# Convolution results of later chunks kept in DRAM, adapter weights brought on chip before the adapters

## The chip, the core and the metric

The kernel runs on one core of one Trainium2 chip. The core has a matrix engine (PE; PEld is its weight load), a vector engine (DVE), an activation engine (ACT), a general engine (POOL) and SP, which here only issues DMAs. DMAs are issued on the queues of SP, ACT and POOL, each of which takes its instructions in order, and all of them run on the same 16 DMA engines. The metric is the device time of one execution in microseconds (us).

## The reference

Four residual layers are applied one after the other to x of shape (32, 64, 1024), in float32. Cut to what matters:

```python
x = x + L0(x)   # per channel h: causal convolution with K_h of 1024 taps, plus D_h * x; masked by length
x = x + einsum('bsi,boi->bso', x, W1[id1])   # one 1024 x 1024 adapter out of 16 for each batch
x = x + einsum('bij,bkj->bik', x, W2[id2])   # and a second one
x = x + L3(x)   # gated FFN, 1024 -> 2752 -> 1024, each product with a rank-16 addition by id3
...
K = 2.0 * einsum('hn,hnl->hl', Ct, exp(dtA[:, :, None] * arange(length))).real
...
gate = lora_add(einsum('bnh,fh->bnf', x, W_gate), x, A_gate, B_gate)
up = lora_add(einsum('bnh,fh->bnf', x, W_up), x, A_up, B_up)
act = silu(gate) * up
down = lora_add(einsum('bnf,hf->bnh', act, W_down), act, A_down, B_down)
```

The batch is 32 rows b with 64 tokens (h in the first layer) of 1024 values. The first layer convolves along the 1024 values, for each h with a kernel of its own, for all 32 rows at once; the later layers multiply along them.

## The kernel before

**Tiling.** x is held transposed, with 128 of the 1024 values on the partitions: a tile `[128, 8, 512]` holds one chunk of 8 batch rows (2 MB), and there are four chunks c = 0 to 3. The convolution works on all chunks at once, four channels (`ha`) at a time; everything after it goes chunk by chunk.

**Convolution** (`convolution`). `kernels(g)` computes the taps of eight channels on DVE, ACT and POOL, PE multiplies them together (`pk`), POOL adds D in the `ks` row (L754) and ACT writes them to DRAM (`kp`). `convolve` loads `uf` (the reversed x of four channels, 512 KB) and twice `hk` (overlapping rows of the taps of two channels, 1 MB, three buffers) on SP, PE makes 64 matmul instructions of them (L782, `pc`), DVE masks the result into `tmp`, and POOL adds `tmp` into the four chunks of x with four instructions (L798). All four chunks are therefore loaded at the start (L581) and lie on chip through the convolution; the last two lie in `x2pool`.

**Adapters** (`adapter`, `adapters`). A piece is one layer of one batch row: eight weight tiles of 512 KB (`early` or `wa`, kt = 0 to 7) are loaded on SP, PE makes 16 matmul instructions with each (L176, `pa`), DVE transposes the sum and adds it to x (L187, L189). A chunk has 16 pieces. Layer 1 of row b stands in front of layer 2 of row b - 1. The row's weight index is read by SP into a register; the read for a piece is held behind the loads of four pieces before. The tiles of chunk 0 first take `early` (nine tiles of their own) and then `wpool`, a pool of nine slots that the weights of the FFN share. `issue_after(blocks[5])` holds the first three pieces' loads behind the sixth `hk` load; after that the scheduler places them among the `hk` loads by its own estimate.

**FFN** (`ffn`, `gated`). For each chunk, hidden columns are worked off in blocks of six and five tiles m. A tile m has two halves g (gate and up, weights `wg` and `wu`), each of seven products on PE (L367, `pf`), with a low-rank addition (`pe`, L309) from rows gathered by POOL (`bgu`, L214). After each half, `between(i)` with i = 2m + g is called; it calls `other`, which gives out the 16 adapter pieces of the next chunk in even shares between the FFN's products, so that their weight loads run beside FFN work. After each block come the products of the down projection (L507, `po`), with weights `wd`. The order on PE is the program's; the scheduler places the instructions of the other engines.

**Chunks.** `xpool` has two x tiles. In the first `between` of chunk 0 POOL writes chunks 2 and 3 to DRAM (`park`, L124), and `x2pool` is given to `apool`, the FFN's activations. In the first `between` of chunk 1 (and 2) SP loads chunk 2 (and 3) back (L454, `x<-xd`) into the tile of chunk 0 (and 1); it waits there until ACT's `out_y` writes of the old chunk have read it.

## Time and profile before

| What | us |
|---|---|
| median of the 3 runs (2449.39 to 2451.61) | 2451.41 |
| the profiled execution's own time | 2448.96 |
| its span | 2447.3 |
| first to last convolution matmul (L782) | 41.5 to 206.4 |
| first to last adapter matmul of chunk 0 (L176) | 206.4 to 371.8 |
| first FFN matmul of chunks 0, 1, 2, 3 | 380.4, 926.5, 1471.5, 2020.1 |

The profile records one execution. Its page gives the busy time of each engine, the busy tenths of the span in 40 slices, the DMA queues with packets, bytes and the share of 16 engines that their packets took, the chain of waits that ended last, and the costliest groups of instructions with the idle time before them and what ended it. Queries of the trace give the same for a window, a tile or a source line; a timeline merges runs of like instructions: start, length, engine, line, operation, count, and in brackets the engine's idle time before and what ended it. `SPq` and `POOLq` are queues, where the time is that of issuing. A granted clock of 1.00 is the full clock of PE.

### The profile page before, as it was taken

Reading aid. Unit: us, or ns where it says so; the run is one execution under the profiler, and the core shown is the slowest. Engines: PE = TensorE matmul, PEld = TensorE weight load, DVE = VectorE, ACT = ScalarE, POOL = GpSimd, SP = SyncE. Lnnn points to the kernel's source line nnn. Section 1 sums busy time; section 2 is a strip of 40 time slices with the busy share of each in tenths; the row PEclk is TensorE's granted clock in tenths of the full one; section 3 lists DMA queues with packets and bytes.
Section 4 is the critical chain, followed back from the end, with each engine's and each line's share of the span. In section 5 each row is a group of like instructions: output and inputs, shape, how many; then the busy total and the mean of one; then the engine's idle time right before and its main releaser. Section 6 shows DMA issues by size and latency. Waiting matters only on the chain.

```text
span 2447.3 us, 47048 instructions
## 1 busy us (share of the span) xinstructions
PE 2353.5 (96%) x19488; PEld 1877.8 (77%) x19488; DVE 1166.1 (48%) x2264; ACT 313.2 (13%) x613; POOL 204.0 (8%) x286
## 2 busy tenths in 40 slices
PE   3898888999999999999999999999999999999999
PEld 3896336888877787877877787878877788888887
DVE  8811114544345544544344544544354545654554
ACT  3200002111011101110011101110011102110110
POOL 3533001000000020000000020000000020000000
PEclk9999999999999999999999999999999999999999
DMA  6789998565567547565566547565566543323221
GB/s 238 253 292 366 408 408 336 190 236 168 190 224 254 181 146 266 209 217 182 175 244 231 179 152 258 207 216 190 177 244 218 184 149 113 89 76 111 87 65 61
DMA packets 162967, 501.24 MB, mean 205 GB/s; under 512 B 19842, under 2 KB 53954, under 8 KB 161730
## 3 DMA queue, kind: packets, MB, share of 16 engines
q1 hardware_dynamic: 146338, 461.76, 54.2%
q0 software_dynamic: 9504, 27.80, 3.4%
q10 hardware_dynamic: 6912, 8.69, 1.0%
q8 instruction: 153, 2.51, 0.4%
q14 instruction: 60, 0.49, 0.1%
HBM read 485.29 MB, written 12.88 MB: 204 GB/s over the span
## 4 chain that ended last, share of the span: by engine, by line
PE 87%; issue 6%; DMA 3%; DVE 2%; POOL 0%; POOLq 0%; SPq 0%; ACT 0%; DVEq 0%; ACTq 0%
PE pf L367 43%; PE po L507 22%; PE pa L176 14%; PE pc L782 5%; PE pe L309 2%; PE pl_d L266 1%; PE po L292 1%; DMA x<-xd 1%; DMA early<-in_w 0%; DMA wf<-in_wu 0%; POOL x L798 0%; DMA out_y<-x 0%; DMA hk<-kp 0%; DMA raw_g<-in_ag 0%; DMA ln<-in_lens 0%
## 5 line engine op out<-in xcount | busy, mean ns | idle before, releaser
L367 PE MATMUL pf<-xd,wf 128*128 128x256 f32 (+1 forms) x2816 | 667.3, 381 | 0.0
L367 PEld LDWEIGHTS pf<-xd,wf 128*128 128x128 f32 (+1 forms) x2816 | 523.0, 187 | 89.1 <-issue 7.5
L176 PE MATMUL pa<-wa,x 128*32 128x256 f32 x8048 | 472.5, 384 | 33.9 <-DMA wa<-in_w 26.7
L367 PE MATMUL pf<-xd,s 128*128 128x256 f32 (+1 forms) x2112 | 499.2, 379 | 2.9 <-ACT c L383 1.7
L367 PEld LDWEIGHTS pf<-xd,s 128*128 128x128 f32 (+1 forms) x2112 | 395.8, 188 | 63.6 <-ACT c L383 2.1
L176 PEld LDWEIGHTS pa<-wa,x 128*32 128x32 f32 x8048 | 249.5, 111 | 249.8 <-DMA wa<-in_w 67.4
L507 PE MATMUL po<-act,wd 128*128 128x256 f32 x704 | 177.0, 385 | 0.0
L507 PE MATMUL po<-actd,s 128*128 128x256 f32 x704 | 172.9, 379 | 0.0
L507 PE MATMUL po<-actd,wd 128*128 128x256 f32 x704 | 172.9, 379 | 0.0
L782 PE MATMUL pc<-uf,hk 128*128 128x256 f32 (+7 forms) x1024 | 153.4, 313 | 17.0 <-DMA hk<-kp 16.7
L214 POOL DMA_INDIRECT bgu<-in_bgu,rows x44 | 45.9, 1044 | 1431.7 <-PE pe L309 1428.2
L782 PEld LDWEIGHTS pc<-uf,hk 128*128 128x128 f32 x1024 | 148.8, 196 | 21.3 <-DMA hk<-kp 9.6
L392 DVE TENSOR_TENSOR c<-pf,u 128x256 f32<-128x256 f32 (+1 forms) x88 | 37.4, 425 | 266.3 <-PE pf L367 266.3
L507 PEld LDWEIGHTS po<-act,wd 128*128 128x128 f32 x704 | 130.6, 190 | 28.0 <-issue 10.2
L507 PEld LDWEIGHTS po<-actd,s 128*128 128x128 f32 x704 | 133.6, 190 | 18.4
L507 PEld LDWEIGHTS po<-actd,wd 128*128 128x128 f32 x704 | 133.6, 190 | 18.4
L319 ACT COPY lt<-pe 128x512 f32<-128x512 f32 (+1 forms) x176 | 90.3, 598 | 372.8 <-PE pe L309 268.9
L337 DVE TENSOR_TENSOR s<-wf 128x512 f32<-128x512 f32 x88 | 59.9, 681 | 119.7 <-DMA wf<-in_wu 44.9
L396 DVE TENSOR_TENSOR c<-c,lt 128x1024 f32<-128x1024 f32 (+1 forms) x88 | 107.7, 1224 | 6.7
L187 DVE STREAM_TRANSPOSE y<-pa 128x512 f32<-128x512 f32 x64 | 45.5, 711 | 137.1 <-PE pa L176 137.1
L337 DVE TENSOR_TENSOR s<-wd 128x384 f32<-128x384 f32 x64 | 33.4, 521 | 137.5 <-PE po L507 97.4
L388 DVE TENSOR_TENSOR c<-pf,c 128x256 f32<-128x256 f32 (+1 forms) x88 | 37.3, 424 | 105.4 <-PE pf L367 105.2
(150 smaller groups left out, 1713.6 us busy)
## 6 DMA issues: line engine op xcount, KB each, us to landing
wa<-in_w SPq DMA_DIRECT2D x503, 512.0 KB, 7.6
wf<-in_wg SPq DMA_DIRECT2D x88, 512.0 KB, 4.4
wf<-in_wu SPq DMA_DIRECT2D x88, 512.0 KB, 5.2
wd<-in_wd SPq DMA_DIRECT2D x96, 384.0 KB, 4.5
hk<-kp SPq DMA_DIRECT2D x32, 1024.0 KB, 7.9
x<-in_xt SPq DMA_DIRECT2D x4, 2048.0 KB, 10.6
uf<-in_xf SPq DMA_DIRECT2D x16, 512.0 KB, 6.1
wd<-in_wd SPq DMA_DIRECT2D x32, 256.0 KB, 3.4
```

The lines of the kernel that those rows point to most:

```text
L176: nc.tensor.matmul(acc[i * S : (i + 1) * S, s * 256 : (s + 1) * 256], xs[c][:, kt, lo + s * S : lo + (s + 1) * S], wt[:, i * 256 : (i + 1) ...
L187: nc.vector.transpose(y, acc)
L214: nc.gpsimd.indirect_dma_start(out=t, out_offset=None, in_=table, in_offset=bass.IndirectOffsetOnAxis(ap=rows[:, c, piece : piece + 1], axis=0
L309: nc.tensor.matmul(ps[:n, at_ : at_ + 2 * H], bt[pair(j), g, i, :n], tms["gu"[g]][pair(j)], start=(g + i == 0), stop=True, skip_group_chec ...
L319: nc.scalar.copy(lt[:n, :, 2 * H * j : 2 * H * (j + 1)], ps[:n].rearrange("p (i t) -> p i t", i=4),)
L337: nc.vector.tensor_add(s1, a21, a22)
L367: nc.tensor.matmul(ps, ws[j][:, kt, :n], xb[j][:, kt, :], start=start and kt == 0, stop=kt == KH - 1, skip_group_check=True,)
L388: nc.vector.tensor_add(cq[:n, 3], pb, cq[:n, 3])
L392: nc.vector.tensor_add(cq[:n, 1], pb, u[:n])
L396: nc.vector.tensor_add(cf, cf, lt[:n, g].rearrange("p i t -> p (i t)"))
L507: nc.tensor.matmul(pss[j], ws[j][:k, i, :], ab[m - m0][j], start=(m == m0 and home[j] % 2 == 0), stop=(m == m1 - 1), skip_group_check=True,)
L782: nc.tensor.matmul(ps[:, j, d * B :], hk[:, j, d * P : (d + 1) * P], uf[:, i + j, : KT - d, :].rearrange("p k b -> p (k b)"), start=(d == ...
```

## The change

Chunks 1 to 3 are no longer loaded at the start. For each four channels POOL adds the convolution's result into chunk 0 only; the results of the other three chunks are copied by POOL into `co` (768 values per partition) and written by POOL's queue to `cd` in DRAM, in rows of 256 values. When a chunk's turn comes, `bring` loads its x from the input (2 MB, SP) and its results in four tiles `cv` of 512 KB that take slots of `wpool`; POOL adds them to x in 16 instructions. `bring` is called in two parts, in `between(0)` and `between(1)` of the chunk before, and `other` gives out the 16 pieces from `between(2)` on. `park` and the reload are gone.

The adapter loads become one stream (`weights`) in the order of the pieces. `fetch` draws from it: at `ha` = 0 the 20 tiles that have places of their own (16 in `early`, four in the x tile that chunk 1 takes later), and from `ha` = 12 on one more for each four channels, until nine more stand in `wpool`: 29 in all. The ids are loaded first on SP. `apool` is opened before the FFN.

In the built program SP's order at the start is: ids, `par`, `cst`, `ln`, x of chunk 0, the first `uf`, 20 weight tiles, and then the first `hk`. Of the nine later tiles three stand around the `hk` loads of `ha` = 4, and one each near those of `ha` = 24, 28, 32, 36, 40 and 44. At the start of chunks 1 and 2, SP issues two `wg`, two `cv`, two `wu`, two `cv`, one `wg`, x, one `wg`, and then the first eight `wa`, of which the first four wait for POOL. POOL has the gather of the second `bgu` ahead of the 16 adds there; for chunk 1 (in the FFN of chunk 0) it stands behind the first four adds, and four of the eight `raw_d` loads of the second block stand behind the first eight.

```diff
-EARLY = 9
+EARLY = 16
+HA = 4
...
-    def x_tile(pool, c, tag):
-        return pool.tile([P, KT, TC], F32, tag=tag, name=f"x{c}")
+    def x_tile(c):
+        return xpool.tile([P, KT, TC], F32, tag="x", name=f"x{c}")
     ctx.enter_context(tc.manual_schedule(engines={PE}))
-    xs = [x_tile(xpool, c, "x") for c in range(2)]
-    right = ExitStack()
-    x2pool = right.enter_context(tc.tile_pool(name="x2pool", bufs=1, side="right"))
-    first = right.enter_context(ExitStack())
+    place = x_tile("_early")
+    xs = [x_tile(0)]
+    first = ExitStack()
     epool = first.enter_context(tc.tile_pool(name="epool", bufs=1, side="right"))
-    late = [x_tile(x2pool, c, f"x{c}") for c in range(2, NCK)]
     early = [epool.tile([P, L], F32, tag=f"e{i}", name=f"early{i}") for i in range(EARLY)]
-    blocks = convolution(tc, cst, consts, xt, xf, ssm, lens, xs + late, ps_tile)
-    parked = []
-    def park():
-        for c, x_c in enumerate(late, 2):
-            d = dpool.tile([P, KT, TC], F32, tag=f"xd{c}", name=f"xd{c}")
-            nc.gpsimd.dma_start(d, x_c)
-            parked.append(d)
+    early += [
+        place[:, i : i + L // TC].rearrange("p k t -> p (k t)")
+        for i in range(0, KT, L // TC)
+    ]
+    cd = dpool.tile([NCK - 1, P, H // HA, HA * KT * BC], F32, tag="cd", name="cd")
     ids_sb = cpool.tile([1, 3 * B], I32, tag="ids", name="ids_sb")
     nc.sync.dma_start(ids_sb, ids)
+    loads = []
+    def layers(c):
+        for b in range(c * BC, (c + 1) * BC + 1):
+            if b < (c + 1) * BC:
+                yield 0, b
+            if b > c * BC:
+                yield 1, b - 1
+    def weights():
+        for layer, b in (at_ for c in range(NCK) for at_ in layers(c)):
+            with ExitStack() as after:
+                if len(loads) > 3:
+                    after.enter_context(tc.issue_after(loads[-4]))
+                e = nc.values_load(
+                    ids_sb[0:1, layer * B + b : layer * B + b + 1],
+                    engines=[SP],
+                    min_val=0,
+                    max_val=NE - 1,
+                )
+            for kt in range(KT):
+                name = f"wa{layer}_{b}_{kt}"
+                wt = early.pop(0) if early else wpool.tile([P, L], F32, tag="w", name=name)
+                w = (w1, w2)[layer]
+                load = nc.sync.dma_start(
+                    wt, w[bass.ds(e, 1), kt].rearrange("e p f -> p (e f)")
+                )
+                if kt == KT - 1:
+                    loads.append(load.ins)
+                yield wt
+    stream = weights()
+    ahead = []
+    def fetch(ha):
+        if ha == 0:
+            ahead.extend(next(stream) for _ in range(len(early)))
+        elif ha > HG and len(ahead) < EARLY + 4 + 9:
+            ahead.append(next(stream))
+    convolution(tc, cst, consts, xt, xf, ssm, lens, xs[0], cd, ps_tile, fetch)
+    def bring(c, part):
+        if part == 0:
+            xs.append(x_tile(c))
+            with tc.issue_after(loads[2 * BC - 1]):
+                nc.sync.dma_start(xs[c], xt[:, c])
+        n = H // HA // 4
+        for q in (2 * part, 2 * part + 1):
+            t = wpool.tile([P, n, HA * KT * BC], F32, tag="w", name=f"cv{c}_{q}")
+            nc.sync.dma_start(t, cd[c - 1][:, q * n : (q + 1) * n])
+            for g in range(n):
+                h = (q * n + g) * HA
+                xv = xs[c].rearrange("p k (b h) -> p k b h", h=H)[:, :, :, h : h + HA]
+                tv = t[:, g].rearrange("p (i k b) -> p k b i", k=KT, b=BC)
+                nc.gpsimd.tensor_tensor(xv, xv, tv, ALU.add)
...
-    def adapter(w, layer, b):
+    def adapter(layer, b):
         c, lo = b // BC, (b % BC) * H
-        with ExitStack() as after:
-            if len(loads) > 3:
-                after.enter_context(tc.issue_after(loads[-4]))
-            e = nc.values_load(
-                ids_sb[0:1, layer * B + b : layer * B + b + 1],
-                engines=[SP],
-                min_val=0,
-                max_val=NE - 1,
-            )
         acc = ps_tile(f"pa{layer}_{b}")
         for kt in range(KT):
-            name = f"wa{layer}_{b}_{kt}"
-            wt = early.pop(0) if early else wpool.tile([P, L], F32, tag="w", name=name)
-            load = nc.sync.dma_start(
-                wt, w[bass.ds(e, 1), kt].rearrange("e p f -> p (e f)")
-            )
+            wt = ahead.pop(0) if ahead else next(stream)
...
     def adapters(c):
-        for b in range(c * BC, (c + 1) * BC + 1):
-            if b < (c + 1) * BC:
-                yield adapter(w1, 0, b)
-            if b > c * BC:
-                yield adapter(w2, 1, b - 1)
-    with tc.issue_after(blocks[5]):
-        pieces = adapters(0)
-        for _ in range(3):
-            next(pieces)
-    for _ in pieces:
+        for layer, b in layers(c):
+            yield adapter(layer, b)
+    for _ in adapters(0):
         pass
     first.close()
...
-        def other(share, of=2 * FM * AT_GATED + (2 * KH - 3) * AT_DOWN):
+        def other(share, of=2 * (FM - 1) * AT_GATED + (2 * KH - 3) * AT_DOWN):
             due[0] += share * NPIECE
             while due[1] * of < due[0]:
                 next(others, None)
                 due[1] += 1
         def between(i):
-            if i == 0 and c == 0:
-                with tc.issue_after(cols[-1]):
-                    park()
-                right.close()
-                apools.append(
-                    ctx.enter_context(
-                        tc.tile_pool(
-                            name="apool", bufs=MB, side="right", reuse_waits="tile"
-                        )
-                    )
-                )
-            if i == 0 and c and c + 1 < NCK:
-                x_n = x_tile(xpool, c + 1, "x")
-                nc.sync.dma_start(x_n, parked[c - 1])
-                xs.append(x_n)
-            other(AT_GATED)
+            if i < 2:
+                if c + 1 < NCK:
+                    bring(c + 1, i)
+            else:
+                other(AT_GATED)
...
-def convolution(tc, cst, consts, xt, xf, ssm, lens, xs, ps_tile):
+def convolution(tc, cst, consts, xt, xf, ssm, lens, x0, cd, ps_tile, fetch):
...
-        for c in range(NCK):
-            nc.sync.dma_start(xs[c], xt[:, c])
+        nc.sync.dma_start(x0, xt[:, 0])
...
         def convolve(kp, row, ha):
-            uf = s3.tile([P, 4, KT, B], F32, tag="uf", name=f"uf{ha}", bufs=2)
-            nc.sync.dma_start(uf, xf[:, ha : ha + 4])
-            tmp = s2.tile([P, 4, KT * B], F32, tag="tmp", name=f"tmp{ha}")
-            for i in range(0, 4, 2):
+            uf = s3.tile([P, HA, KT, B], F32, tag="uf", name=f"uf{ha}", bufs=2)
+            nc.sync.dma_start(uf, xf[:, ha : ha + HA])
+            fetch(ha)
+            tmp = s2.tile([P, HA, KT * B], F32, tag="tmp", name=f"tmp{ha}")
+            for i in range(0, HA, 2):
...
-            tv = tmp.rearrange("p i (k b) -> p k b i", b=B)
-            for c in range(NCK):
-                xv = xs[c].rearrange("p k (b h) -> p k b h", h=H)[:, :, :, ha : ha + 4]
-                nc.gpsimd.tensor_tensor(xv, xv, tv[:, :, c * BC : (c + 1) * BC, :], ALU.add)
+            xv = x0.rearrange("p k (b h) -> p k b h", h=H)[:, :, :, ha : ha + HA]
+            tv = tmp.rearrange("p i (k b) -> p k b i", b=B)[:, :, :BC, :]
+            nc.gpsimd.tensor_tensor(xv, xv, tv, ALU.add)
+            co = s2.tile([P, NCK - 1, HA * KT, BC], F32, tag="co", name=f"co{ha}")
+            tv = tmp.rearrange("p i (k c b) -> p c (i k) b", k=KT, b=BC)[:, 1:]
+            nc.gpsimd.tensor_copy(co, tv)
+            nc.gpsimd.dma_start(
+                cd.rearrange("c p g e -> p c g e")[:, :, ha // HA],
+                co.rearrange("p c i b -> p c (i b)"),
+            )
```

## The prediction

> **What bounds the kernel now.** I read the busy shares first, then the windows by stage, then the timelines of the SP queue and of PE around the places that the diff touches.
>
> ```profile
> PE 2353.5 (96%) x19488; PEld 1877.8 (77%) x19488; DVE 1166.1 (48%) x2264; ACT 313.2 (13%) x613; POOL 204.0 (8%) x286
> DMA  6789998565567547565566547565566543323221
> ```
>
> 96% is an average over unlike stages. The windows below (columns: window, length, busy time of PE, PEld, DVE, ACT, POOL, then granted clock, DMA share, GB/s) separate them.
>
> ```profile
> 150.00:190.00 40.00, 39.97 (x298) 38.93 (x295) 6.00 (x9) 0.72 (x2) 14.44 (x20) 1.00 0.86 287
> 240.00:280.00 40.00, 33.42 (x502) 13.41 (x504) 5.63 (x8) 0.00 (x0) 0.00 (x0) 1.00 1.03 408
> ```
>
> The convolution (150 to 190 us) is bound by PE, with the DMA engines at 0.86. The first adapters (206 to 371 us) are bound by transfers: 408 GB/s at a DMA share of 1.03, and that is the ceiling I use. The FFN stages afterwards are PE again. The weight stream of the first adapters, and its last tile:
>
> ```profile
> 193.27 5.51 SPq L171 DMA_DIRECT2D early<-in_w  x7
> 201.53 159.38 SPq L171 DMA_DIRECT2D wa<-in_w  x119
> 370.72 1.07 PE L176 MATMUL pa<-wa,x 128*32 128x256 f32 x16 [0.21 <-DMA wa<-in_w]
> ```
>
> Only 2 of the 9 `early` tiles are issued before 193 us (117.7 and 155.7 in the SP timeline); 126 of the 128 tiles of 512 KB cross in this one stage. Two further holes in PE are the reloads of chunks 2 and 3:
>
> ```profile
> 941.42 7.11 PE L176 MATMUL pa<-wa,x 128*32 128x256 f32 x128 [2.59 <-DMA x<-xd]
> 1487.16 9.94 PE L176 MATMUL pa<-wa,x 128*32 128x256 f32 x128 [3.31 <-DMA x<-xd]
> ```
>
> The second piece also takes 9.94 instead of 7.11 us: the window 1470 to 1500 has a granted clock of 0.89, so the wait cost 3.3 us and another 2.9.
>
> **The change, part by part**, against the profiled execution's own 2448.96 us (span 2447.3, 1.7 around it).
>
> *A, 29 tiles ahead.* A tile takes 524,288 B / 408 GB/s = 1.285 us of DMA; a piece of 128 matmuls is 7.04 us in the chain of waits, so PE eats a tile in 0.88 us. In the new order of SP, 20 loads stand before the first `hk`, 9 more between the `hk` of ha = 4 and ha = 44. PE begins the adapters at 208.2 us as now (it waits there for the last add to chunk 0). The other 99 tiles need `wpool`'s 9 slots, which hold tiles 20 to 28; the first slot comes free when PE has passed tile 20, at 208.2 + 21 x 0.88 = 226.7. So the stream restarts at 226.7 instead of running on from 193.3: 126 tiles become 99 (27 x 1.285 = 34.7 saved), 33.4 us of early start are given up, and the gathers and low-rank loads that share the stream now (24% of it from 215 to 232 us), the last `hk` and ring slots not yet free lose their price, because they fall before the restart. Counted directly: first tile landed about 3.3 us after 226.7, then 98 x 1.285, gives 356; now 370.7. **-14** (bounds -11, if 3 us of today's disorder return, and -16).
>
> *B, chunk 1's first two pieces moved behind the first hidden tile.* Now chunk 0's first `m` runs from 380.44 to 422.62: 42.2 us, of which 24.4 + 2 x 7.04 = 38.5 is work; the weights `wu` are issued at 394.8, behind 8 `wa`. In the new order they follow 2 `wg`, `x1` and 2 `cv`: 10 units of 512 KB, some 13 us after the last adapter tile, and PE asks for them some 22 us after it. **-3** (0 to -3.7).
>
> *C, x brought in two parts, adapters one `m` later.* The x load still waits for the `out_y` writes (issue at 933.51 now, landing 7.8 us later). The first piece of the next chunk now runs 12.3 + 12.3 + 1.1 + 12.3 = 38 us after the chunk's start at 926.5, at 964.2. Before it, POOL must make 16 adds, rows of
>
> ```profile
> L798 POOL TENSOR_TENSOR x<-x,tmp x64: 828/858/1631, 58.0 to 209.7; 128x256 f32<-128x256 f32 x64
> ```
>
> from 941.3: 16 x 0.858 = 13.7, ready at 955; at the mean of that group (0.924) 956. 8 us to spare, so both waits go: 2.6 + 3.3 + 2.9 = **-8.8**. Queued behind: on POOL the gather of the next `bgu`, which stands ahead of the adds for chunks 2 and 3, and after four of them for chunk 1 (wanted by PE 20 us later); on SP the first four `wa`, which wait for POOL to release the `cv` slots, and behind them `wu` of m = 1 (needed at 971). Four of nine slots are held until 955, so I put +1 for small waits (0 to +7). The 12 `cv` and 3 x loads (12 MB) replace 4 MB of reload and 6 MB at the start, and the 4 MB parked from POOL's queue: these stages run at DMA shares of 0.5 to 0.7, so the cover is PE; without it the 24 units of 512 KB, against 8 of the reload, would cost 16 x 1.285 / 3 = 6.9 us a chunk. If x is late again, the first piece of the chunk is what waits.
>
> *D, POOL in the convolution.* Four adds become one add, one copy of 768 elements and a DMA issue. This POOL work is on the path once, where PE idles for the second kernel (7.2 us):
>
> ```profile
> 58.00 4.58 POOL x L798 x4
> 62.58 0.23 POOL ks L754
> 62.83 1.53 DMA kp<-ks
> 64.38 6.16 DMA hk<-kp
> ```
>
> No row shows a POOL copy. Between one 256-element operation with contention (1.15) and three of them uncontended (2.57) or contended (3.45): I take 2.5, as 768 elements are three of these rows. 1.15 + 2.5 = 3.65 for 4.58: **-0.9** (-2.3 to 0). The DMA issue stands behind the `ks` add.
>
> *E, the convolution's transfers.* Per four channels (9.25 us of PE) `hk` and `uf` take 0.855 x 9.25 = 7.9 us of DMA less the share of other queues, some 7.7. Six of the periods get a tile (+1.29), all get a 393 KB store in 384 rows of 1 KB. Its price is not in the trace; the rows around it are the queues of ACT's `out_y` (872 to 890 us) and of POOL's small loads (215 to 232 us); the columns are packets, MB, share:
>
> ```profile
> q10 hardware_dynamic: 288, 0.52, 7.6%
> ```
>
> ```profile
> q0 software_dynamic: 602, 1.55, 24.2%
> ```
>
> 7.6% of 18 us x 16 engines / 288 is 76 ns for 1.8 KB, the other 109 ns for 2.6 KB; by bytes alone 1 KB is 0.96 us a store, at 109 ns it is 2.6. Stores in 2 KB rows are nearest: scaled by size, some 46 ns, 1.1 us. 7.7 + 1.29 + 1.1 = 10.1 against a ceiling of 1.026 x 9.25 = 9.5: 0.6 x 6 = 3.6, less the 1.3 us by which an `hk` (lands in 7.9) is ahead of its use (two halves, 9.2): **+2.3** (0 to +19). The 20 loads, 10.5 MB from some 9 us on at 408 GB/s, end near 36 us, about when the first `hk` is issued (35.34): **+0.5** (0 to +8, at the 238 GB/s of the first slice).
>
> [...]
>
> [...]
>
> **Sum:** -14 - 3 - 8.8 + 1 - 0.9 + 2.3 + 0.5 = -22.9: 2426.1 us. The profiled execution is 2.45 below the median of the runs shown (2451.41) and 0.4 below the lowest (2449.39); I add 1 and say **2427**.
>
> **Rivals.**
> 1. *The convolution becomes bound by transfers.* A store costs 109 ns a row, 2.6 us: the six periods with a tile take 11.6 instead of 9.5 (+12.6), the other nine 10.3 (+7), less 1.3: +18 in place of +2.3, **2443**. For it: the share is 0.86 already. Against: 109 ns is of rows twice as long or more.
> 2. *The 20 loads hold up the first `hk`* (the slice's 238 GB/s): +8 instead of +0.5, **2435**. For it: nothing else can shift 41.5 us. Against: that slice was not saturated (share 0.6).
> 3. *The slower one: POOL's adds gate the chunk.* They are now between x's landing and the first piece, and hold four of nine weight slots, with SP waiting behind them. At t us an add they end at 941.3 + 16t, and `wu` lands some 10 us later (7 tiles); PE wants it at 971.3, so there is slack up to t = 1.25. At the row's maximum (1.63) each of two chunks loses 6 us and 2.9 of clock: 18 in all, still a little faster. From t = 1.8 the loss passes 22.9 and the change is slower; at t = 2.3 each loses 17 + 2.9: **2466**. For it: the same adds rose to 1.63 beside a busy DVE. Against: DVE was 97% busy there and is 48% here, and from 100 us on they average 0.885.
> 4. *The change doesn't do what it says*: the 9 later tiles get no slot before the adapters. 9 x 1.285 less the earlier restart: within 5 us of the forecast, so it has no chance of its own.
>
> **How the numbers follow.** Forecast 0.70 (2416 to 2438 from the bounds of A to D and of E up to a 1.6 us store); rival 1 0.12; rival 2 0.06; rival 3 0.12. The range 2414 to 2446 holds the forecast, rival 2 and half of rival 1. A measurement here tells 0.2% (4.9 us) from no change: faster means below 2446.5. Faster 0.70 + 0.06 + 0.08 = 0.84; same 0.04 from rival 1's upper half; slower 0.12.
>
> **What would show it.** A: SP issues 20 tiles before 35 us; DMA drops well under 0.9 between 206 and 227 us; the last adapter matmuls start near 357. B and C: no `x<-xd`; the first piece of chunks 2 and 3 without a wait on DMA or POOL, at full clock; adds near 0.9 us. D: the gap near 63 us shorter by 1. E: PE still without gaps from 92 us on, a store's share near 0.12 of a period. I am wrong if PE waits for `hk` in the convolution, or if `pa` in the second `m` waits for POOL.

## The result and the profile after

The change made the kernel slower: 2464.03 us median (2451.45 to 2466.67, 19 runs) against 2449.39 (2446.83 to 2452.13, 19 runs) beside it on the same chip, a ratio of the means of 1.0052 (95% interval 1.0042 to 1.0062). The profiled execution took 2457.69 us (span 2456.0), 8.7 more than the one before; it is one of the five faster ones of the 19 (2451 to 2458; the other 14 lie at 2462 to 2467). What sets the 14 apart is found further down, at e5; why two runs lie as low as 2451 and 2453 is not.

The stages, read from PE's timeline in both profiles (the first matmul of each kind), tell where the 8.7 us are (differences are of the unrounded times):

| Stage | before | after | difference |
|---|---|---|---|
| start to first convolution matmul | 41.5 | 47.7 | +6.2 |
| first to last convolution matmul | 164.9 | 170.2 | +5.2 |
| end of convolution to first FFN matmul | 174.0 | 162.5 | -11.5 |
| chunk 0, 1, 2 (first FFN matmul to the next chunk's) | 546.0, 545.0, 548.6 | 550.9, 548.1, 549.1 | +4.8, +3.1, +0.6 |
| chunk 3 and the rest | 427.2 | 427.5 | +0.2 |

From the page, the busy times and the DMA share by slice:

```profile
PE 2353.7 (96%) x19488; PEld 1880.5 (77%) x19488; DVE 1174.0 (48%) x2264; ACT 315.6 (13%) x615; POOL 233.5 (10%) x316
...
DMA  8796996665665646665666646656656643323221
```

The same windows as before, with one more where the stream pauses:

```profile
150.00:190.00 40.00, 38.25 (x289) 37.14 (x288) 5.54 (x8) 0.72 (x2) 9.82 (x14) 1.00 0.93 340
206.00:237.00 31.00, 29.88 (x417) 22.23 (x419) 6.22 (x13) 1.04 (x1) 14.04 (x22) 1.00 0.37 125
240.00:280.00 40.00, 34.04 (x537) 14.88 (x532) 7.73 (x11) 0.00 (x0) 0.00 (x0) 1.00 1.02 398
```

In the convolution PE is busy 38.25 of 40 us instead of 39.97, with the DMA engines at 0.93. From 206 to 237 us they are at 0.37: the 29 tiles are there. From SP's timeline, the tiles ahead of the first `hk` and the restart:

```profile
8.50 18.05 SPq L153 DMA_DIRECT2D early<-in_w  x16
27.51 11.99 SPq L153 DMA_DIRECT2D x_early<-in_w  x4
39.97 0.91 SPq L794 DMA_DIRECT2D hk<-kp  x2
...
237.59 123.28 SPq L153 DMA_DIRECT2D wa<-in_w  x99
```

The first `hk` is issued at 39.97 instead of 35.34. From PE's timeline, three stretches of the convolution and the last adapter tile (which stood at 370.72 before):

```profile
47.74 11.40 PE L805 MATMUL pc<-uf,hk 128*128 128x256 f32 x64 [13.92 <-DMA hk<-kp]
...
78.49 20.58 PE L805 MATMUL pc<-uf,hk 128*128 128x256 f32 x128 [8.79 <-DMA hk<-kp]
...
109.66 9.36 PE L805 MATMUL pc<-uf,hk 128*128 128x256 f32 x64 [0.66 <-ACT bsq L633]
...
370.67 1.07 PE L221 MATMUL pa<-wa,x 128*32 128x256 f32 x16 [0.21 <-DMA wa<-in_w]
```

The last adapter tile stands where it stood: the convolution ended 11.4 us later and the adapters took 11.5 less. The waits of `pa` for `x<-xd` (2.59 and 3.31 us) are gone, and new ones stand at the start of chunks 0, 1 and 2. The timeline around the first, with ACT, POOL and DVE:

```profile
388.12 3.27 POOL L188 TENSOR_TENSOR x<-x,cv 128x256 f32<-128x256 f32 x4
388.46 1.47 ACT L281 COPY at_d<-raw_d 128x1536 f32<-128x1536 f32 x1 [5.93 <-DMA raw_d<-in_ad]
389.83 0.37 ACT L417 COPY u<-pf 128x256 f32<-128x256 f32 x1
390.10 0.38 ACT L419 COPY c<-pf 128x256 f32<-128x256 f32 x1
390.51 1.18 DVE L420 TENSOR_TENSOR u<-c,u 128x256 f32<-128x256 f32 x1 [9.63 <-ACT c L419]
...
390.53 3.78 PE L403 MATMUL pf<-xd,s 128*128 128x256 f32 x8 [4.69 <-ACT c L419]
```

PE waits 4.69 us for ACT's copy of a product out of PSUM, the memory that PE writes its products to; ACT, in order, has the copy of the down adapter ahead of it, and that waits 5.93 us for `raw_d`. The same two lines in the profile before:

```profile
385.50 1.47 ACT L245 COPY at_d<-raw_d 128x1536 f32<-128x1536 f32 x1 [2.92 <-DMA raw_d<-in_ad]
...
387.57 1.99 PE L367 MATMUL pf<-xd,s 128*128 128x256 f32 x8 [1.69 <-ACT c L383]
```

After the change the eight matmuls behind the wait take 3.78 instead of 1.89 us: the granted clock is 0.5 for 6.8 us. In chunk 1 another chain leads to the same place (the last line is chunk 2's):

```profile
938.58 0.33 SPq L179 DMA_DIRECT2D x<-in_xt  x1
940.18 0.33 SPq L398 DMA_DIRECT2D wf<-in_wg  x1
...
945.76 16.88 POOL L188 TENSOR_TENSOR x<-x,cv 128x256 f32<-128x256 f32 x16 [13.09 <-DMA x<-in_xt]
...
946.92 1.04 DVE L373 TENSOR_TENSOR s<-wf 128x512 f32<-128x512 f32 x1 [4.59 <-DMA wf<-in_wg]
...
951.03 1.06 ACT L438 ACTIVATE act<-c 128x1024 f32<-128x1024 f32 x1 [5.30 <-DVE c L432]
...
952.40 3.21 PE L403 MATMUL pf<-xd,s 128*128 128x256 f32 x8 [3.62 <-ACT c L419]
...
1500.02 3.78 PE L403 MATMUL pf<-xd,s 128*128 128x256 f32 x8 [3.11 <-ACT c L419]
```

SP's load of x waits 8.7 us for the `out_y` writes with the second half of a weight pair behind it. DVE, in order, waits 4.59 us for that half, and then its operations run beside 16 adds of POOL and take longer (L373 1.04 us; 0.68 without them). ACT's sigmoid waits 5.30 us for DVE, and the product copy stands behind it.

### The profile page after: what moved, and what is told of

Read it like the earlier page. It is cut to its first block, busy times and chain, and to the rows that moved or that the text cites. A ratio compares the mean times of both kernels' runs of the same rounds, so it can differ in the third digit from the quotient of the medians.

```text
span 2456.0 us, 47094 instructions
## 1 busy us (share of the span) xinstructions
PE 2353.7 (96%) x19488; PEld 1880.5 (77%) x19488; DVE 1174.0 (48%) x2264; ACT 315.6 (13%) x615; POOL 233.5 (10%) x316
## 4 chain that ended last, share of the span: by engine, by line
PE 85%; issue 7%; DVE 4%; DMA 3%; POOL 1%; POOLq 0%; ACT 0%; SPq 0%; DVEq 0%; ACTq 0%
PE pf L403 43%; PE po L532 22%; PE pa L221 14%; PE pc L805 3%; PE pe L345 2%; PE pl_d L302 1%; DMA kp<-ks 1%; DMA hk<-kp 1%; PE po L328 1%; DMA wf<-in_wg 1%; DMA ln<-in_lens 0%; DVE bk L625 0%; DVE bsp L619 0%; PE pl_u L302 0%; PE pl_g L302 0%
## 5 line engine op out<-in xcount | busy, mean ns | idle before, releaser
L403 PE MATMUL pf<-xd,s 128*128 128x256 f32 (+1 forms) x2112 | 504.2, 382 | 11.5 <-ACT c L419 11.4
L221 PE MATMUL pa<-wa,x 128*32 128x256 f32 x7872 | 454.8, 381 | 22.0 <-DMA wa<-in_w 20.7
L221 PEld LDWEIGHTS pa<-wa,x 128*32 128x32 f32 x7872 | 242.0, 110 | 227.4 <-DMA wa<-in_w 57.0
L805 PEld LDWEIGHTS pc<-uf,hk 128*128 128x128 f32 x1024 | 148.4, 195 | 31.4 <-DMA hk<-kp 14.1
L428 DVE TENSOR_TENSOR c<-pf,u 128x256 f32<-128x256 f32 (+1 forms) x88 | 37.3, 424 | 267.2 <-PE pf L403 267.2
L532 PEld LDWEIGHTS po<-act,wd 128*128 128x128 f32 x704 | 130.3, 190 | 29.1 <-issue 11.4
L373 DVE TENSOR_TENSOR s<-wf 128x512 f32<-128x512 f32 x88 | 61.5, 699 | 115.1 <-DMA wf<-in_wg 43.7
L432 DVE TENSOR_TENSOR c<-c,lt 128x1024 f32<-128x1024 f32 (+1 forms) x88 | 109.6, 1246 | 6.7
L373 DVE TENSOR_TENSOR s<-wd 128x384 f32<-128x384 f32 x64 | 33.3, 521 | 141.8 <-PE po L532 96.9
L424 DVE TENSOR_TENSOR c<-pf,c 128x256 f32<-128x256 f32 (+1 forms) x88 | 37.3, 424 | 103.8 <-PE pf L403 103.5
```

Source lines behind the costliest of these rows:

```text
L221: nc.tensor.matmul(acc[i * S : (i + 1) * S, s * 256 : (s + 1) * 256], xs[c][:, kt, lo + s * S : lo + (s + 1) * S], wt[:, i * 256 : (i + 1) ...
L373: nc.vector.tensor_add(s1, a21, a22)
L403: nc.tensor.matmul(ps, ws[j][:, kt, :n], xb[j][:, kt, :], start=start and kt == 0, stop=kt == KH - 1, skip_group_check=True,)
L424: nc.vector.tensor_add(cq[:n, 3], pb, cq[:n, 3])
L428: nc.vector.tensor_add(cq[:n, 1], pb, u[:n])
L432: nc.vector.tensor_add(cf, cf, lt[:n, g].rearrange("p i t -> p (i t)"))
```

## The experiments

The theories. **T1**: the convolution loses what the adapters gain, by the 20 tiles ahead of the first `hk` and by the stores or the later tiles slowing small transfers. **T2**: the chunk starts lose, because a late transfer (`raw_d`, a weight half behind x) or POOL's adds hold an in-order engine between PE and PSUM. The table has all runs, each with the kernel before beside it on its chip; the columns on the right are from PE's timeline of its one profile (us). "c0, c1, c2" are the chunks from first FFN matmul to first FFN matmul.

| Run | median (range, runs) | before | ratio, 95% | first, last convolution matmul | first FFN matmul | c0, c1, c2 |
|---|---|---|---|---|---|---|
| e1 unaltered | 2457.2 (2456.3 to 2467.6, 6) | 2448.6 | 1.0027 to 1.0060 | 46.7, 217.6 | 379.8 | 550.7, 549.8, 549.6 |
| e2 no later tiles | 2456.6 (2450.0 to 2464.8, 10) | 2448.6 | 1.0024 to 1.0052 | 47.7, 216.9 | 379.8 | 550.2, 548.3, 549.4 |
| e3 no stores | 2453.3 (2446.7 to 2461.9, 10) | 2448.6 | 1.0009 to 1.0038 | 48.0, 212.6 | 375.1 | 550.8, 548.5, 548.7 |
| e4 twelve first | 2453.7 (2448.5 to 2459.6, 10) | 2448.6 | 1.0007 to 1.0033 | 43.9, 211.7 | 373.6 | 550.7, 548.5, 548.3 |
| e5 copy later | 2464.1 (2459.9 to 2466.2, 4) | 2450.2 | 1.0037 to 1.0075 | 48.6, 217.3 | 379.9 | 556.6, 549.6, 549.8 |
| e6 no adds | 2444.4 (2441.8 to 2445.6, 10) | 2450.2 | 0.9965 to 0.9984 | 47.0, 219.0 | 381.5 | 550.0, 542.6, 542.8 |
| e7 bring one m later | 2449.8 (2446.9 to 2451.0, 10) | 2450.2 | 0.9988 to 1.0008 | 47.7, 218.0 | 380.5 | 551.0, 544.7, 544.7 |
| e8 two kernels ahead | 2452.3 (2448.2 to 2456.5, 10) | 2450.2 | 0.9999 to 1.0019 | 46.7, 211.9 | 374.4 | 556.6, 548.2, 548.5 |
| e9 second raw | 2466.5 (2465.1 to 2467.6, 4) | 2449.9 | 1.0050 to 1.0084 | 47.9, 217.1 | 384.1 | 557.5, 548.2, 548.9 |
| e10 adds on DVE | 2462.2 (2462.1 to 2464.5, 4) | 2449.9 | 1.0037 to 1.0072 | 48.2, 217.4 | 380.7 | 549.5, 550.7, 552.3 |
| e11 three mended | 2446.0 (2442.6 to 2449.0, 10) | 2449.9 | 0.9976 to 0.9995 | 42.5, 208.9 | 375.8 | 548.4, 544.6, 545.0 |
| e12 four mended | 2443.6 (2441.9 to 2446.4, 9) | 2449.9 | 0.9969 to 0.9989 | 44.4, 210.9 | 377.3 | 550.8, 544.7, 544.8 |
| e13 raw and DVE | 2458.6 (2457.9 to 2460.0, 5) | 2448.6 | 1.0027 to 1.0056 | 47.8, 217.0 | 383.8 | 543.4, 551.7, 552.3 |
| e14 all and DVE | 2452.5 (2449.2 to 2454.3, 10) | 2448.6 | 1.0002 to 1.0021 | 44.5, 210.0 | 376.6 | 544.2, 551.1, 552.0 |
| e15 DVE for chunk 1 | 2438.1 (2437.7 to 2438.7, 4) | 2448.8 | 0.9936 to 0.9969 | 44.1, 209.3 | 375.6 | 544.2, 545.1, 544.6 |

### The convolution: e1 to e4, e8

> The changed kernel again, unaltered, as the yardstick of this chip and as a second profile of it. In its first profile (span 2456.0 us) the first convolution matmul stood at 47.7 us, the last convolution matmul ended at 217.9, the last adapter matmul of chunk 0 at 370.7, and PE waited 4.7, 3.6 and 3.1 us for ACT's copy of a gated product at the start of chunks 0, 1 and 2. That profile was one of the faster runs (2457.7 against a median of 2464.0). Theory 1 (the convolution's transfers come late) expects a slower run to show a later last convolution matmul; theory 2 (chunk starts: ACT and DVE wait for a transfer in order, and PE waits for them) expects the difference of 6 us to lie at the starts of chunks 0 to 2, with more time at the half granted clock.

On this chip five of six runs lie at 2456 to 2459 and one at 2467.6. The profile is of the lower kind and repeats the first one within a us, so it doesn't show what the upper kind has; e5 does.

```diff
-        elif ha > HG and len(ahead) < EARLY + 4 + 9:
-            ahead.append(next(stream))
```

> The nine adapter tiles that are fetched between the groups of the convolution are fetched after it; the 20 at its start stay. If these tiles are what slows the small transfers (kp lands in 9 to 10 us instead of 2.7), kp lands in under 5 us here, the gaps of PE between 100 and 165 us (4.3 us) are gone and the convolution takes 166 us from first to last matmul instead of 170. If the stores of the convolution results are it, kp still takes 9 us and the convolution 170. In both cases the nine tiles have to come later, at 1.28 us each: 11.5 us, less the 4 that the first theory gives back, so the last adapter matmul stands near 378 by the first and near 382 by the second, and the whole is 7 or 11 us above the changed kernel.

A miss of both theories, by 7 to 11 us. From SP's timeline of this run:

```profile
123.78 0.43 SPq L153 DMA_DIRECT2D wa<-in_w  x1
...
162.20 0.39 SPq L153 DMA_DIRECT2D wa<-in_w  x1
...
204.30 156.01 SPq L153 DMA_DIRECT2D wa<-in_w  x104
```

The edit did less than it says. The scheduler still put four of the nine tiles into the convolution (issued at 55, 59, 124 and 162 us) and the other five right behind the last `hk`, from 204 us on, while PE still works on the convolution; the last line runs them together with the 99 of the restart. They are there when the `early` ones are used up, and the stream restarts as before. With five tiles fewer the convolution takes 169.2 us instead of 170.2 and 170.9, and `kp` lands in 8.5 us, not under 5: these five hardly stretch it. For all nine the next run tells more.

```diff
-            nc.gpsimd.dma_start(
-                cd.rearrange("c p g e -> p c g e")[:, :, ha // HA],
-                co.rearrange("p c i b -> p c (i b)"),
-            )
...
-            nc.sync.dma_start(t, cd[c - 1][:, q * n : (q + 1) * n])
+            nc.sync.dma_start(t.rearrange("p a b -> p (a b)"),
+                xt[:, c, 2 * q : 2 * q + 2].rearrange("p k t -> p (k t)"))
```

> The 16 stores of convolution results to DRAM are left out; the later loads of the same size read x instead, so that chunks 1 to 3 get x twice and not the convolution: transfers and instructions after the convolution are as before. If the stores slow kp and hk, kp lands in under 5 us, the convolution takes 166 us instead of 170 and the whole is about 4 us less than the changed kernel. If the tiles do, kp still lands in 9 us, and the whole is within 1 us of it. The prediction's price for the stores (2.3 us) would have the whole 2.3 less.

The convolution takes 164.7 us, as before the change (164.9), with all nine tiles still in it, and the median falls by 3.9: the stores (with the 0.8 us of POOL that issuing each takes) are what stretches it, and the tiles alone don't. From the DMA issues between 41 and 218 us (size, median us from issue to landing), the kernel before first, then the changed one, then this run:

```profile
kp<-ks ACTq DMA_DIRECT2D x7, 32.0 KB, 2.7
```

```profile
hk<-kp SPq DMA_DIRECT2D x30, 1024.0 KB, 8.3
...
cd<-co POOLq DMA_DIRECT2D x15, 384.0 KB, 7.2
...
kp<-ks ACTq DMA_DIRECT2D x7, 32.0 KB, 10.0
```

```profile
hk<-kp SPq DMA_DIRECT2D x30, 1024.0 KB, 7.5
...
kp<-ks ACTq DMA_DIRECT2D x7, 32.0 KB, 6.9
```

`kp` is 32 KB in rows of 128 B, and SP's next `hk` waits for it. Without the stores it still takes 6.9, not under 5 as expected, yet PE has no gap over 0.4 us from 78 us on. That the 3.1 us less for `kp` and 0.8 for `hk` are what closes the gaps is the likely reading; no run tries it apart from the share of the DMA engines that the stores take.

```diff
-            ahead.extend(next(stream) for _ in range(len(early)))
-        elif ha > HG and len(ahead) < EARLY + 4 + 9:
+            ahead.extend(next(stream) for _ in range(12))
+        elif len(ahead) < EARLY + 4:
+            ahead.extend(next(stream) for _ in range(2))
+        elif len(ahead) < EARLY + 4 + 9:
             ahead.append(next(stream))
```

> Of the 20 tiles ahead of the first hk, 12 stay (with x of chunk 0 as many bytes as the kernel before loads there), the other 8 come two at a time at the next four groups, the nine later ones one at a time as before. If the 20 loads hold up the first hk, the first convolution matmul stands at 42 us instead of 47.7. If the rest of the convolution has room for the 8, its end moves as much, to about 212, the last adapter matmul to 365 and the whole is 5 to 6 us below the changed kernel. If the convolution has no room (its transfers set its pace, DMA share 0.93 to 0.96), the end stays at 217 and the gain is under 1 us.

From PE's timeline of this run:

```profile
43.92 11.43 PE L807 MATMUL pc<-uf,hk 128*128 128x256 f32 x64 [10.45 <-DMA hk<-kp]
...
69.89 21.26 PE L807 MATMUL pc<-uf,hk 128*128 128x256 f32 x128 [3.98 <-DMA hk<-kp]
```

The start comes 3 to 4 us earlier, not 5.7; the gap of the second kernel shrinks from 8.8 to 4.0; the end is at 211.7 and the first FFN matmul 6.2 us earlier. The median falls by 3.5 only, since five of its ten runs lie some 8 us higher (2456 to 2460, by their times the upper kind of e5); the other five lie at 2448.5 to 2451.2, some 7 below e1's lower kind. The 20 loads do hold up the first `hk`, by 3 to 4 of the 6.2 us, and the convolution has room for eight of them.

```diff
-        ready = [kernels(0)]
+        ready = [kernels(0), kernels(1)]
...
-            if len(ready) < H // HG and (ha == 0 or ha % HG == HA):
+            if len(ready) < H // HG and ha % HG == HA:
```

> The second group's kernels are computed right behind the first group's, ahead of the first products, not behind their masks. In the changed kernel (and in the one before) PE waits 7.2 to 10.3 us near 64 to 70 us for the hk of that second group, whose kernels DVE only ends then, because it starts them behind the masks of the first products, and these come 6.2 us later in the changed kernel since the 20 tiles lie ahead of the first hk. If this is how the late first hk is passed on, the gap falls below 2 us, the half clock of 10 us behind it is gone too, the first convolution matmul stays at 46 to 48, the last stands near 206 and the whole is 8 to 12 us less. If the second group's hk would come late anyway for its transfers, the gap stays over 5 us.

The gap near 64 to 70 us is gone, and the end moves from 217.6 to 211.9, half of the 12 us hoped for, since new gaps stand later: 3.5 us at 87, which an operation of DVE ends, and four of 0.9 to 1.8 further on, which `hk` ends. So DVE's order makes the gap of the second kernel, and later waits, for `hk` and once for DVE, take half of the gain back. Its chunk 0 is 556.6 us long, which leads to e5.

### The chunk starts: e5 to e7, e9, e10, e13

> Only the place of ACT's copy of the down adapter (at_d from raw_d) is changed: it stands behind the second gated block instead of ahead of the first. In the changed kernel's profiles PE waits 4.7 us in the first products of chunk 0 for ACT's copies of products, which stand behind that copy, which waits 5.9 us for raw_d. Theory 2 (a late transfer, passed on by an engine's order, and then the half clock): that gap is gone in chunk 0 (at most 0.5 us left), so is the half clock of 6.8 us behind it, and chunk 0 takes 546 instead of 550.8 us; chunks 1 and 2, which wait for another thing, are as they were. The whole is 4 to 8 us less. Rival (PE waits for something else at that place, and the copy is merely what the profile names): the gap stays at 4 to 5 us.

The edit changed nothing: the scheduler put ACT's copy back to the same place, and the program differs from the changed kernel's in line numbers alone. So it is a second repeat, and its profile is of the upper kind. Its span is 5.8 us longer than e1's, and its only new gap, behind the known one in chunk 0, is 5.74 us long. From its timeline, and behind it the same place in e1's (whose line numbers are smaller by 4):

```profile
393.37 7.30 DVE L380 TENSOR_TENSOR s<-wf,s 128x512 f32<-128x512 f32 x1
393.70 6.41 POOL L188 TENSOR_TENSOR x<-x,cv 128x256 f32<-128x256 f32 x8
...
400.60 0.41 DVE L428 TENSOR_TENSOR c<-pf,c 128x256 f32<-128x256 f32 x1
...
401.06 3.50 PE L407 MATMUL pf<-xd,s 128*128 128x256 f32 x8 [5.74 <-DVE c L428]
```

```profile
393.25 0.68 DVE L376 TENSOR_TENSOR s<-wf,s 128x512 f32<-128x512 f32 x1
393.69 7.50 POOL L188 TENSOR_TENSOR x<-x,cv 128x256 f32<-128x256 f32 x8
```

One operation of DVE, which takes 0.68 us otherwise, took 7.30, from just before a run of eight adds on POOL to just after it; DVE's next add, for which PE waits, came that much later. In e1 the same operation started 0.44 us ahead of POOL's run, was through in 0.68, and POOL's eight adds took 7.50. In e5, e8 and e9 POOL began 0.33, 0.42 and 0.33 us behind it, and it took 7.30, 7.40 and 7.35. That is the upper kind of run: e10 and e13, without POOL's adds, have neither the long operation nor the wide spread.

```diff
-                nc.gpsimd.tensor_tensor(xv, xv, tv, ALU.add)
+                if q + g == 0:
+                    nc.gpsimd.tensor_tensor(xv, xv, tv, ALU.add)
```

> Of POOL's 16 adds of a chunk's convolution result to x, 15 are left out (the loads stay, so chunks 1 to 3 lack most of the convolution). If POOL's adds are what makes the first blocks of chunks 1 and 2 slow (DVE's operations beside them take 1.04 to 1.86 us instead of 0.68 to 1.23), the gap of 3.6 to 3.9 us for ACT's copy in chunk 1 shrinks below 2 and chunks 1 and 2 take 2 to 3 us less each. If SP's order is (the load of x waits for the store of y, and the second half of a weight pair behind it comes 4.9 us late to DVE), the gaps shrink by under 1.5 us, for DVE's four faster operations, and the whole by 2 to 3. By the prediction's rival 3 (POOL's adds gate the chunk), 10 us and more are won.

Chunks 1 and 2 take 542.6 and 542.8, without a gap, 7 us less each than in e1, and the runs lie within 3.8 us of each other. It doesn't part the two causes, since the scheduler also put the load of x three transfers later on SP, behind the weight half. Together they are the whole of what chunks 1 and 2 lost. The median lies 12.8 below e1's, and 19.8 below that of e5, the unaltered program on the same chip (2460 to 2466). That is as much as rival 3 of the prediction would have, but not by its way: chunk 0's second gap is gone as well.

```diff
-            if i < 2:
+            if i in (2, 3):
                 if c + 1 < NCK:
-                    bring(c + 1, i)
-            else:
+                    bring(c + 1, i - 2)
+            elif i > 3:
                 other(AT_GATED)
```

> x and the convolution tiles of the next chunk are brought one block later (in the second gated block instead of the first), and the next chunk's adapters are spread over one block less. In chunks 1 and 2 the load of x then no longer waits for the store of y with a weight tile of the second block behind it; in chunk 0 the burst of x and four tiles no longer lies beside the raw_d loads. Theory 2: the gaps of 4.7, 3.6 to 3.9 and 3.1 to 3.8 us at the starts of chunks 0, 1 and 2 fall below 2, 1 and 1, with the half clock behind them; chunks 0, 1 and 2 take 547, 545 and 545 us, and the whole is 8 to 13 us less, near 2446. If the gaps only move to where the bringing now stands, the chunks keep 549 to 551 us and the whole is within 3 us of the changed kernel. If the adapters, with less room, become late, a gap stands at the end of a chunk, at a wait for wa.

Chunks 1 and 2 take 544.7 as expected. SP's load of x is issued at the same time, and a weight half still stands behind it (at 940.37 in chunk 1), but it is one of `wu`, which DVE takes up at 954.5 and 955.2 without a wait. Of the adds a gap of 1.2 us is left in each chunk. Chunk 0 misses (551.0 for 547): `raw_d` lands as late without the `cv` tiles beside it, and PE waits 4.74 us for it. The median lies 7.4 us below e1's (14.3 below e5's, on the same chip), at that of before.

```diff
-        raw = gpool.tile([P, BC, n, R], F32, tag="raw", name=f"raw_{name}", bufs=1)
+        raw = gpool.tile([P, BC, n, R], F32, tag="raw", name=f"raw_{name}", bufs=2)
...
-    ypool = ctx.enter_context(tc.tile_pool(name="ypool", bufs=2, reuse_waits="tile"))
+    ypool = ctx.enter_context(tc.tile_pool(name="ypool", bufs=1, reuse_waits="tile"))
```

> A second buffer for the raw adapters (the room comes from a second buffer of y that is given up), so that the loads of raw_d no longer wait for ACT's copy of raw_u and are issued some 140 us earlier; ACT's copy of at_d then finds them there. The earlier try to put that copy later left it where it was. Theory 2: the gap of 4.6 to 4.7 us in chunk 0, in which PE waits for ACT's product copies behind at_d, is gone, with the half clock of 6.8 us behind it: 5 to 8 us less in chunk 0, unless DVE takes over: POOL's first eight adds then lie beside DVE's adds of products (L420 and L422), and in two profiles one operation of DVE took 7.3 and 7.4 us, from just before to just after eight adds of POOL. If DVE is held so, a gap of 3 to 6 us for DVE stands in the same place and the whole falls by less than 3 us.

The wait for `raw_d` is gone, yet chunk 0 is the longest of all, and all four runs lie at 2465 us or more. From its timeline:

```profile
387.83 3.28 POOL L188 TENSOR_TENSOR x<-x,cv 128x256 f32<-128x256 f32 x4
387.90 0.37 ACT L419 COPY c<-pf 128x256 f32<-128x256 f32 x1 [1.34 <-PE pf L403]
388.31 3.09 DVE L420 TENSOR_TENSOR u<-c,u 128x256 f32<-128x256 f32 x1 [3.67 <-ACT c L419]
...
392.03 4.09 DVE L374 TENSOR_TENSOR s<-s,wf 128x512 f32<-128x512 f32 x1
392.29 3.27 POOL L188 TENSOR_TENSOR x<-x,cv 128x256 f32<-128x256 f32 x4
...
397.29 7.35 DVE L376 TENSOR_TENSOR s<-wf,s 128x512 f32<-128x512 f32 x1
397.62 6.47 POOL L188 TENSOR_TENSOR x<-x,cv 128x256 f32<-128x256 f32 x8
...
405.04 3.78 PE L403 MATMUL pf<-xd,s 128*128 128x256 f32 x8 [11.99 <-DVE c L424]
```

Three operations of DVE lie under three runs of POOL's adds and end with them. PE's gap is 12.0 us, longer than the 3 to 6 expected: the wait for `raw_d` had stood in the place of the first two. The adapters of chunk 0 also took 4 us longer here (158.4 us for 153.9), as in e11 to e15; whether for the earlier raw loads beside the weights or the single y buffer wasn't tried.

```diff
-                nc.gpsimd.tensor_tensor(xv, xv, tv, ALU.add)
+                nc.vector.tensor_tensor(xv, xv, tv, ALU.add)
```

> The 16 adds of a chunk are given to DVE instead of POOL, in the same place of the program. If POOL's run of adds is what holds DVE (L376 took 7.3 us in one profile and 0.68 in another), no operation of DVE takes over 2 us in the first block of chunk 0, the second gap of 5.7 us, which stood in two of eight profiles, doesn't occur, and the runs of this kernel lie within 5 us of each other instead of 10 to 15. The adds are 16 at about 0.42 us, 7 us of DVE. In chunks 1 and 2 they stand in DVE's order ahead of the adds of products and wait there for x, which lands near 945: PE should wait longer there than the 3.6 to 3.9 us of the changed kernel, by 3 to 7 us a chunk. Rival (the operation is held by a transfer or by its own operands): operations of 7 us occur here too.

As expected: no long operation, no second gap, four runs within 2.5 us. In chunks 1 and 2 PE waits 6.1 and 7.1 us while DVE waits for x, 2 to 3 us longer than in e1, not 3 to 7; these chunks are 1 and 3 us longer, and the median lies above e1's lower kind.

> A second raw buffer and the adds on DVE, both on the changed kernel. With the second raw buffer alone PE waited 12.0 us in chunk 0 for DVE, one operation of which took 4.1 and one 7.4 us beside runs of four and eight adds on POOL; with the adds on DVE alone it waited 4.8 us for ACT behind raw_d. If POOL's adds are what held DVE, no operation of DVE takes over 2 us here, the gaps at the start of chunk 0 sum to under 1.5 us, chunk 0 takes 543 to 546 us (before: 546.0; with the raw buffer alone 557.5, with the adds on DVE alone 549.5), and the whole is 4 to 6 us under the 2462 of the adds on DVE alone; chunks 1 and 2 keep their 550 to 552. If DVE was held by something else (a transfer, its operands), a gap of over 4 us stands there again and chunk 0 takes 549 or more.

Its edits are those of e9 and e10 together. From its timeline, the same place of chunk 0:

```profile
384.17 4.25 DVE L188 TENSOR_TENSOR x<-x,cv 128x256 f32<-128x256 f32 x8
...
387.32 1.89 PE L403 MATMUL pf<-xd,wf 128*128 128x256 f32 x8
...
389.05 1.89 PE L403 MATMUL pf<-xd,s 128*128 128x256 f32 x8
...
390.93 0.69 DVE L376 TENSOR_TENSOR s<-wf,s 128x512 f32<-128x512 f32 x1
```

PE has no gap at all there, L376 is back at 0.69 us, and chunk 0 takes 543.4 us: 14.1 less than e9, which differs in the engine of the adds alone. The two waits are the whole of what chunk 0 lost; no third stands behind them. The whole is 3.6 us under e10, not 4 to 6, since the adapters of chunk 0 took 3 us more, as in e9.

### Mended versions: e11, e12, e14, e15

These put together e4, e7 and e9 (e11), e8 as well (e12), all adds on DVE as well (e14), and, last, the adds of chunk 1 alone on DVE:

```diff
-                nc.gpsimd.tensor_tensor(xv, xv, tv, ALU.add)
+                (nc.vector if c == 1 else nc.gpsimd).tensor_tensor(xv, xv, tv, ALU.add)
```

> Three edits together on the changed kernel: twelve tiles ahead of the first hk and eight in the next groups, the bringing of x one block later, a second raw buffer. Twelve first won 3.5 us in the medians, bringing later 7.4 against the changed kernel's 2457.2, the third is worth 4.7 to 8 where nothing takes its place (bringing later has taken POOL's first adds away from that place). If the causes add up, the whole stands at 2457 - 3.5 - 7.4 - 6 = 2440, 10 us below the kernel before; if the third gives nothing, at 2446.

> The same three with the kernels of the second group computed ahead of the first products. By itself that moved the end of the convolution from 217.6 to 211.9 us. With twelve first the gap it removes is 4.0 us and its half clock 6.8 instead of 8.8 to 10.3 and 10 to 13.7; the transfers of the convolution, at a DMA share of 0.96 to 0.98 there, leave little room. If DVE's order was the limit, 4 to 6 us less than the three alone, near 2435; if the transfers are, within 2 us of the three.

> The four mended (2443.6) and the adds on DVE. In its profile chunk 0 lost 4.2 us to a gap, and 3.4 to the half clock behind it, after DVE operations of 3.8 and 1.2 to 1.9 us beside POOL's adds; chunks 1 and 2 a gap of 1.2 each. If POOL's adds cause these, and x and cv are there when DVE comes to the adds, chunk 0 takes 544 to 546 instead of 550.8 and the whole stands near 2438. If DVE has to wait for x or cv in its order, gaps of 3 us and more stand in the second block of the chunks, and the whole is at 2444 to 2452.

> The four mended, with the adds of chunk 1 alone (made during the FFN of chunk 0, where x and cv are on chip in time) on DVE, and those of chunks 2 and 3 on POOL. From the run with all adds on DVE chunk 0 takes 544.2 us, from the four mended with POOL chunks 1 and 2 take 544.7 and 544.8, against 550.8 in chunk 0 of the four mended: 6.6 us less than its 2443.6, so 2437, 12 us below the kernel before. If POOL's adds at chunks 1 and 2 depend on something that the place in chunk 0 changes, 2441 to 2444.

e11 gave 2446.0, what it was to give if the second raw buffer brings nothing: POOL's adds take the place of `raw_d` in chunk 0 (548.4 us, a gap of 3.85). e12 gave 2443.6, 2.4 us less than e11 and not the 4 to 6 of "DVE's order" alone; in the profiles the convolution takes as long in both (166.4 and 166.5 us), and of e12's gaps in it `hk` ends the longest. e14 gave 2452.5, since DVE waits for x in chunks 1 and 2 (gaps of 6.2 each), while chunk 0 takes the 544.2 expected. e15 has each mend where it helped: 2438.06 against an expected 2437, 0.9953 of the kernel before (0.9936 to 0.9969). So the causes in the chunks add up once each mend stands where nothing takes its place, and the change with its side effects mended beats the kernel before by 10.7 us. A part of that could perhaps be had without the change: the second kernel ahead, and the second raw buffer, since PE waited 1.69 us there before, too. That wasn't tried.

## Why the prediction was wrong

It said 2427 (2414 to 2446), and the median is 2464. The profile has 31 of the 37 us between them (the sum was -22.9, the profile has +8.7); the other 6 are the upper kind of run. By its own steps, against the profile:

- **A** held: -11.5 for -14, near its lower bound of -11. The stream restarted 19.7 us behind the first adapter matmul (237.6), where the working had 18.5; but the convolution itself ended 11.4 us later, which eats the gain exactly.
- **The 20 loads** (+0.5, 0 to +8) were mis-sized: +6.2, which is rival 2. The step put their end near 36 us, from 408 GB/s; the window from 0 to 41 us moved 321 GB/s in the profile (267 before). e4 gives back 3 to 4 of it; where the rest comes from is open, and the first kernel product (`pk`) already stands 1.8 us later (32.76 for 30.95). The upper bound isn't what its rate gives: at 238 GB/s, 10.5 MB take 44 us, 18 more than at 408 and not 8.
- **D** (-0.9) didn't show: the second kernel's gap is 8.8 us for 7.2, though POOL's copy of 768 elements was cheaper than taken (0.90 us on average for 2.5). Without the stores (e3) the gap is 6.7, so it is likely the stores that take this gain, and by e8 it is DVE's order that makes the gap.
- **E**, the stores and tiles (+2.3, 0 to +19): +5.2 with D's gap, by e3 all of it the stores'; the nine tiles are in e3 as well. Their DMA time was priced rightly: between 41 and 218 us POOL's queue took 8.6% of 16 engines for 15 stores, 1.0 us of all engines each, for 1.1. What the step left out is, most likely, latency: it looked whether the engines had room in a period, and `kp` on ACT's queue, with an `hk` in order behind it, landed in 10.0 us instead of 2.7. Rival 1 (109 ns a row, +18) was wrong in its price.
- **B** (-3) failed: chunk 0 lost 4.8 in the profile and 10.6 in the upper kind of run. The step asked when the weights come and not what else stands in order between PE and PSUM: ACT's copy behind `raw_d`, then DVE behind POOL's adds. The gain itself was there: with both waits gone (e13) chunk 0 takes 543.4 us, 2.6 less than before.
- **C** (-8.8, +1): the two waits went, as it said, and chunks 1 and 2 together still took 3.7 us more, not 7.8 less. The sum looked at the adds from x's side (done at 955, wanted at 964.2): they ended at 962.6, and no `pa` waited for POOL. They took DVE with them, and the load of x took a weight half with it (e7: back to 544.7; e6, which leaves out 15 of the 16 adds: 542.6 and 542.8 without both, together 8.2 less than before, about what C had promised).
- **Rival 3** gave 2466 and slower, and its place was right, POOL's adds in the first blocks; its mechanism (SP and the adapters behind the adds) was not. The adds cost 1.03 us on average, below its threshold of 1.8.

So the steps that failed most are B and C, the starts of the chunks: -10.8 forecast, +8.5 measured, 19 of the 31 us. Both asked when the weights and x land, and put at nothing what stands in an engine's order ahead of the copies that free PSUM. PE waited for such a copy 4.7, 3.6 and 3.1 us in the three chunks of the profile, for `raw_d` in chunk 0 and for the weight half and POOL's adds in the other two; in the upper kind of run it waited 5.7 us more in chunk 0, for DVE behind POOL alone.

No sum of the prediction has a price for what POOL's adds do to DVE, though the profile before has an operation of DVE that took longer beside POOL: L603 at 30.82 us took 0.83 us beside L716 and L717 of POOL, where the median of the eight of its kind was 0.425. In e5 it was not one POOL instruction of 0.8 us but a run of eight that DVE was held for, 7.3 us in all, although its operation had started 0.33 us ahead of POOL by the profile. That POOL's adds are the cause is shown by e9 against e13 (7.35 and 0.69 us for L376); how one engine holds the other is not shown.

What stays open: why `raw_d` lands 3 us later than before (not for the `cv` tiles, by e7), what the remaining 2 to 3 us of the late start are, and how the cost at chunks 1 and 2 splits between the order on SP and POOL's adds, beyond the 1.2 us a chunk that e7 leaves.

## What to carry to other kernels

Work given to an idle engine is priced by what it holds up, not by its own time: POOL was 8% busy, and 16 adds of 0.8 us in the wrong place cost up to 12 us of PE through DVE (e9), while eight loads too many ahead of the first `hk` cost 3 to 4 (e4). Before moving a transfer, list for each in-order engine near the new place what stands behind its next wait, down to the copies that free PSUM. And test the parts one at a time: undoing each where it hurt turned +0.5% into -0.5%.

## What the runs showed of the hardware that was not expected

- An operation of DVE that meets a run of back-to-back POOL adds can be held for the whole run (in e9 L420, L374 and L376 took 3.09, 4.09 and 7.35 us beside runs of 4, 4 and 8, and 0.43, 0.69 and 0.69 in e13, without POOL's adds), take 0.3 to 0.7 us longer (L373 to L376, L420, L432 and L439 in chunks 1 and 2 of the changed kernel: 0.4 to 1.2 us became 1.0 to 1.9), or not be held at all. Those with a product of PE among their operands (`c<-pf`: L422, L424, L428, L430) kept 0.41 to 0.43 us beside the same runs in that profile. Ahead of the run of eight L376 (L380 in e5) was held where it had started 0.33 to 0.42 us before POOL (e5, e8, e9), and not where it had started 0.44 us before (e1); the two kinds of runs lie 6 us apart.
- A small write (32 KB in 128-B rows) landed in 2.7 us before the change, 10.0 after it and 6.9 without the stores (medians of seven), while the 1 MB loads took 7.9, 8.3 and 7.5.
- POOL copied 768 elements in 0.90 us on average, as long as its two-operand add of 256 elements in the same stage (0.90).
- Stores of 1 KB rows on POOL's queue appeared as 112 packets of 3.5 KB each, at 145 ns (8.6% of 177 us x 16 engines over 1680 packets).
